# A graph-attention and slice-attention layer on one core: the second MLP as seven block products, the norms inverted as 128x4, the masked logits in one pass, and other turns

## The chip, the cores and the metric

The kernel runs on one core of a Trainium2 chip. The core has five engines with a queue each: TensorE (PE) multiplies matrices into the eight PSUM banks, VectorE (DVE) and ScalarE (ACT) do elementwise work, GpSimd (POOL) does a few small things, and SyncE (SP) issues DMAs. An engine takes its instructions in the order in which they stand in its queue and waits on semaphores for the others. The metric is the device time of one execution in microseconds, lower is better; the median of several runs is given.

## What is computed

The input x has 32 batches of 512 nodes with 256 features, all in float32. One layer has two halves. The first is a graph network with two attention stages; the second, 0/1 adjacency masks only the second stage. The second half is an attention over 64 slices for each of 8 heads. Cut to what matters:

```python
def _gat(inp, adj_mask, W, a):
    h = inp @ W
    f1, f2 = h @ a[:F_, 0], h @ a[F_:, 0]
    e = leaky_relu(f1[:, :, None] + f2[:, None, :], 0.2)
    if adj_mask is not None:
        e = where(adj_mask[None] > 0, e, -9e15)
    return elu(einsum('bij,bjf->bif', softmax(e, axis=2), h))

# first half, on layernorm(x)
out = relu(x @ mlp1_w + mlp1_b)                     # 256 -> 512
out = elu(_gat(out, None, W_fc, a_fc)) + out        # 512
out = relu(out @ mlp2_w + mlp2_b)                   # 512 -> 256: the "second mlp"
out = relu(elu(_gat(out, adj, W_hand, a_hand)) + out)
x = x + out

# second half, on layernorm(x)
w = softmax((x @ W_x @ W_slice) / temp)             # 8 heads x 64 slices
slice_token = einsum('bhnc,bhng->bhgc', x @ W_fx, w) / (w.sum(2)[..., None] + 1e-5)
attn = softmax(q @ k.T * SCALE)                     # from slice_token
x = x + (attn @ v, spread back with w) @ W_out
```

## The kernel before, in words

Each batch is one age of a software pipeline (`nc.age = b`). All its operations are written down by a recorder (`Recorder`) and not emitted at once. `order()` then plays through all 32 ages with a table of costs (`_cost`), and at each step gives every engine the ready operation with the lowest key. The keys come from `TURNS`, one number for each step of a batch (load, norm1, mlp1, h, factors, p, pv, o1, mlp2, h2, e, p2, pv2, norm2, w, sums, s1T, tokens, att, vo, gg, out), with corrections for the first and last three batches in `HEAD` and `TAIL`. The order that comes out is emitted, so that it is fixed when the program is built; up to four batches are under way at a time. All instructions carry the line of the emitting call (L288 in the profile of before), so that groups are told apart by tile names.

A batch has 512 nodes as four tiles of 128 rows. The steps that matter here:

- `h` (line 682): the product of o0T (the first MLP's output, features on partitions) with `wfc` is done as seven block products: four mixtures of o0T in the tile `mix`, three mixtures of the weights in `mixed`, sums of products on DVE into the tile `h`. After it come `factors`, `p` and `pv`: the attention without mask, whose weights lie in `pT`.
- `o1` (line 790): the attention's output goes through DRAM (`gather`: four writes to `scr`, one read of 1 MB) to come back transposed as `o1T`, and o0T is added.
- `mlp2` (line 800): two output tiles of 128 features, each four products of 128x128 weights from `w2` with 512 columns of `o1T`, and one ReLU with bias on ACT into `o2T`.
- `h2` and `e` (lines 810 to 848): `h2` is o2T times `wh`; the two logits columns stand beside it. For each of the four row tiles DVE adds the column logits `f2b`, the row logit and the mask `mbias` (bfloat16), takes the leaky ReLU as max(0.2 e, e), and the row's maximum; ACT takes the exponential. DVE transposes 32x32 blocks into `e_stage`, and a gather through DRAM makes `p2T`.
- `w`, `sums`, `s1T`, `tokens` (lines 908 to 992): w holds the slice weights. `sums` multiplies them with the normalised x, whose last feature is set to 1, so that the last row of `s1T` holds the norms, 512 numbers in one partition. They go to DRAM (`line`) and come back broadcast over partitions as `rn` (128x256), where DVE adds 1e-5 and inverts; `tok` is the tokens' product times `rn`.

A tile that carries a tag shares its buffer with the other tiles of that tag; `bufs` is how many such buffers there are. Each float32 matmul of the program stands as two MATMUL instructions in the profile.

The few lines to have at hand:

```python
pm.rearrange("p (a t i) -> p a t i", t=NT, i=Q), w2[:, k, ts(m)],      # 806
swapped(o1T[:, k, :]), start=(k == 0), stop=(k == KH - 1),              # 807
nc.vector.tensor_scalar(rn, rn, 1e-5, None, op0=OP.add)                 # 974
nc.vector.reciprocal(rn, rn)                                            # 975
```

Of the kernel before, what the change touches and what calls it, by code (L numbers as in the profile page):

```python
# [10 lines left out]
AF = mybir.ActivationFunctionType  # L11
OP = mybir.AluOpType
AX = mybir.AxisListType
# [1 line left out]
ENGINES = ("tensor", "vector", "scalar", "gpsimd", "sync")  # L15

TURNS = {
    "load": -462.5, "norm1": 57.6, "mlp1": 1478.5, "h": 1624.1, "factors": 1626.7, "p": 1631.1,
    "pv": 1644.1, "o1": 1647, "mlp2": 1694.9, "h2": 1709.3, "e": 1714.6, "p2": 1102.3,
    "pv2": 1733.3, "norm2": 1780.6, "w": 1806.7, "sums": 1812.1, "s1T": 1826.8, "tokens": 2321.2,  # L20
    "att": 658.3, "vo": 1004.5, "gg": 1394.8, "out": 1524.2,
}
PERIOD, SPARE = 89.9, 0.01

HEAD = (
    (-33, 108, 3, -726, 0, 63, -4, 93, -317, -118, -101, -31, 114, 36, 581, -77, -43, -443, 55,
     -1, 16, -659),
    (302, 200, 0, 41, 0, 223, 198, 0, -15, 0, 760, -14, -1674, -151, 33, -31, -61, -1067, 191,
     -140, -300, 8),
    (-6, 37, 1179, -81, 0, 0, -1864, -1, 0, 1, -105, -68, -395, 94, 4, -151, 5, 3, -336, 3, 0,  # L30
     0),
)
TAIL = (
    (-203, -62, 1108, 0, -19, -60, 101, 4, -242, -90, -82, 1, -58, -418, -434, 1119, -43, -15,
     -10, 0, -198, 0),
    (295, 0, 75, 221, 12, 158, -7, 50, -1, 64, 0, 173, -8, -61, -5, 0, 30, 0, -59, -299, 730,
     197),
    (94, 1079, -126, 0, -154, 915, -18, 0, 0, -1924, -62, -58, -41, 72, -15, 360, 0, -238, 0,
     -132, -14, 140),
)  # L40


# [3 lines left out]

P = 128
ALPHA = 0.2
MASKED = -4.5e16


class Recorder:
# [3 lines left out]
    SIGNAL = 0.06  # L56
    DRAIN = 0.17
    ISSUE, BEGIN, LAND, BEHIND = 0.45, 2.2, 0.0, 3.6
    SWITCH = 0.1
    KEPT = 1  # L60
    AHEAD = 3

# [65 lines left out]
    def _cost(self, op, out, ins):  # L128


        def words(ap):
            return ap.size() // ap.ap[0][1]

        n = words(out)
        if op.method == "dma_start":
            side = next(ap for ap in (out, *ins) if ap.space != bass.MemoryType.DRAM)
            kb = out.size() / 256
            if side.ap[0][1] <= P // 4:
                op.moving = 0.3 + max(0.0, 1.08 * (kb / 128 - 1))
            else:  # L140
                op.moving = max(1.5 * kb / 512, 4.0 * kb / 1024 - 0.5)
            return self.ISSUE, 0.0
        if op.engine == "tensor":
            one = max(n / 1200 + 0.002, 0.109)
            if op.mode == (P, P // 2):
                one = max(n / 2400, 0.0275)
            elif op.mode == (P // 2, P // 2):
                one = max(n / 4800, 0.0135)
            return (one if op.method == "transpose" else 2 * one), self.DRAIN
        if op.engine == "scalar":  # L150
            pointers = sum(isinstance(op.kwargs.get(k), bass.AP) for k in ("bias", "scale"))
            return 0.06 + n / 1200 + 0.09 * pointers + 0.19 * ("accum_out" in op.kwargs), 0.12
        if op.engine == "vector":
            n = max([n] + [words(x) for x in ins])
            single = op.method in ("tensor_copy", "tensor_scalar")
            fast = single and all(x.space != bass.MemoryType.PSUM for x in ins)
            pointers = sum(words(x) == 1 for x in ins) if n > 1 else 0
            return 0.07 + n / (1920 if fast else 960) + 0.065 * pointers, 0.1
        if n < 16:
            return (0.1 if op.method == "memset" else 0.3 if op.method == "tensor_scalar" else 1.1), 0.1  # L160
        return 0.2 + n / (480 if op.method == "tensor_tensor" else 960), 0.1
# [164 lines left out]
def adj_ffn_kernel(  # L326
# [26 lines left out]
    B, N, D = x.shape  # L353
    HID = mlp1_w.shape[1]
    HH = HID // 2
    NT = N // P
    KD = D // P
    KH = HID // P
# [4 lines left out]
    NP = INNER // P  # L363
    assert G == C == 64 and HEADS * G == 512 and N == 512 and HID == 512 and D == 256

    nc = Recorder(tc.nc)
# [5 lines left out]
    def ts(i, n=P):  # L372
        return slice(i * n, (i + 1) * n)

    def new(name, shape, bufs=1, tag=None, dtype=F32):
        return sbuf.tile(list(shape), dtype, name=name, tag=tag or name, bufs=bufs)

    def mm_tile(shape):
        return psum.tile(shape, F32, tag="bank", name="mm", bufs=8)
# [8 lines left out]
    Q = 32  # L388
# [23 lines left out]
    def swapped(cols):  # L412

        return cols.rearrange("p (t a i) -> p a t i", t=NT, i=Q)
# [4 lines left out]
    def row(name, shape=(P, 512), tag=None):  # L419
        return new(name, shape, bufs=2, tag=tag)  # L420

    def small(name, shape):
        return new(name, shape, bufs=3)
# [8 lines left out]
    def load_x(b):  # L432
# [14 lines left out]
        out=ident, in_=ident, compare_op=OP.not_equal, fill=1.0, base=0,  # L447
# [37 lines left out]
    t1, t2, t4 = (mixed[:, i] for i in range(3))  # L485
    for to, left, right in ((t1, r12, r11), (t2, r22, t1), (t4, r21, t2), (r12, r22, r12)):
        nc.vector.tensor_tensor(to, left, right, op=OP.subtract)
    t3 = r12

    nc.step = "setup"  # L490
    w2 = new("w2", [P, KH, D])
    nc.sync.dma_start(w2, mlp2_w.rearrange("(k p) f -> p k f", p=P))
    b2 = new("b2", [P, KD])
    nc.sync.dma_start(b2, mlp2_b.rearrange("(m p) -> p m", p=P))

# [27 lines left out]
    mbias = new("mbias", [P, NT, N], dtype=BF16)  # L523
# [87 lines left out]
    for p in range(NP):  # L611
        pv = mm_tile([P, D])
# [49 lines left out]
    def front(b):  # L662
# [11 lines left out]
        for m in range(KH):  # L674
            pm = mm_tile([P, N])
# [7 lines left out]

        h = new("h", [P, NT, 2, HH + 1])
        l11, l12, l21, l22 = (o0T[:, ts(k, 2), ts(t, 2 * P)] for t in range(2) for k in range(2))
        mix = new("mix", [P, 4, 2, 2 * P])
        s1, s2, s3, s4 = (mix[:, i] for i in range(4))
        for to, left, op, right in (
            (s1, l21, OP.add, l22), (s2, s1, OP.subtract, l11),
# [32 lines left out]
        f1, f2 = h[:, :, 0, HH], h[:, :, 1, HH]  # L722
# [30 lines left out]
        pT = new("pT", [P, NT, N])  # L753
        for j in range(NT):
# [5 lines left out]
                op0=OP.mult, op1=OP.max,  # L760
# [3 lines left out]
        o1T = new("o1T", [P, KH, N])  # L764
        if by_dma("u", b):
            stage = new("u_stage", [P, HID // Q, P], bufs=2, tag="stage")
        for i in range(NT):
            pms = [mm_tile([P, HH + 1]), mm_tile([P, HH])]
            for s, pm in enumerate(pms):
                for j in range(NT):  # L770
                    nc.tensor.matmul(
                        pm, pT[:, j, ts(i)], h[:, j, s, : HH + 1 - s],
                        start=(j == 0), stop=(j == NT - 1),
# [3 lines left out]
            u, m = row("u"), row("m")  # L777
# [13 lines left out]
        if by_dma("u", b):  # L791
            gather("u", stage, o1T)
            for m in range(KH):
                o1 = o1T[:, m, :].rearrange("p (t a i) -> p t a i", t=NT, i=Q)
# [3 lines left out]
    def middle(b, o1T):  # L798

        nc.step = "mlp2"  # L800
        o2T = new("o2T", [P, KD, N])
        for m in range(KD):
            pm = mm_tile([P, N])
            for k in range(KH):
                nc.tensor.matmul(
                    pm.rearrange("p (a t i) -> p a t i", t=NT, i=Q), w2[:, k, ts(m)],
                    swapped(o1T[:, k, :]), start=(k == 0), stop=(k == KH - 1),
                )
            nc.scalar.activation(o2T[:, m, :], pm, AF.Relu, bias=b2[:, m : m + 1])
        nc.step = "h2"  # L810
        h = new("h2", [P, NT, D + 2], tag="h" if b == B - 1 else None)
        for t in range(NT):
            pm = mm_tile([P, D + 2])
# [5 lines left out]
        f2b = tr_tile([P, N])  # L819
        for j in range(NT):  # L820
            nc.tensor.transpose(f2b[:, ts(j)], h[:, j, D + 1 : D + 2].to_broadcast([P, P]), ident)
        if not by_dma("e", b):
            pt, f2b = f2b, new("f2b", [P, N], tag="acb")
            nc.scalar.copy(f2b, pt)
        nc.step = "e"
        pT = new("p2T", [P, NT, N], tag="pT" if b == B - 1 else None)
        if by_dma("e", b):
            stage = new("e_stage", [P, N // Q, P], bufs=2, tag="stage")
        nmax = small("nmax", [P, NT])
        for i in range(NT):  # L830
            e = new("e", [P, N], bufs=2)
            nc.vector.scalar_tensor_tensor(
                e, f2b, h[:, i, D : D + 1], mbias[:, i, :], op0=OP.add, op1=OP.add
            )
            nc.vector.scalar_tensor_tensor(e, e, ALPHA, e, op0=OP.mult, op1=OP.max)
            nc.vector.tensor_reduce(
                nmax[:, i : i + 1], e, axis=AX.X, op=OP.max, negate=True
            )
            nc.scalar.activation(e, e, AF.Exp, bias=nmax[:, i : i + 1])
            if by_dma("e", b):  # L840
                flip(e, stage[:, :, ts(i, Q)])
                continue
            pt = tr_tile([P, NT, P])
            for j in range(NT):
                nc.tensor.transpose(pt[:, j, :], e[:, ts(j)], ident)
            nc.scalar.copy(
                pT.rearrange("p j (t a i) -> p j t a i", t=NT, i=Q)[:, :, :, i, :],
                pt.rearrange("p j (t i) -> p j t i", i=Q),
            )
# [18 lines left out]
        for i2 in range(NT // 2):  # L868
            parts = []
            for s in range(2):  # L870
                i = 2 * i2 + s
                pm = mm_tile([P, D + 1])
# [7 lines left out]
            u, m = row("u2", (P, 2, D), "u"), row("m2", (P, 2, D), "m")  # L880
# [10 lines left out]
    def back(b, x1):  # L891
# [21 lines left out]
        for t in range(NT):  # L913
            pm = mm_tile([P, INNER])
# [38 lines left out]
        if by_dma("w", b):  # L953
            raw = new("w_raw", [P, NP, N], tag="w")
            gather("w", stage_w, raw)
            for p in range(NP):
                nc.scalar.copy(
                    wT[:, p, :].rearrange("p (t a i) -> p t a i", t=NT, i=Q), swapped(raw[:, p, :])
                )
        nc.step = "s1T"  # L960
        line = dram.tile([NP, 2, G], F32, name="line", tag="line", bufs=2)
        nc.sync.dma_start(
            line.rearrange("(o p) s g -> o (p s g)", o=1), s1T[P - 1 : P, KD - 1, :]
        )
        rn = new("rn", [P, NP, G], tag="mean")
        for s in range(2):
            nc.sync.dma_start(
# [3 lines left out]
                    ap=[[0, C], [2 * G, NP], [1, G]],  # L971
                ),
            )
        nc.vector.tensor_scalar(rn, rn, 1e-5, None, op0=OP.add)
        nc.vector.reciprocal(rn, rn)
        nc.step = "tokens"

        nc.joint = True
# [75 lines left out]
        gg = med("gg")  # L1054
# [93 lines left out]
```

## Time and profile before

| | |
|---|---|
| median of 3 runs | 2535.09 us (2533.92 to 2537.39) |
| the profiled execution | 2531.39 us |
| its span, first to last instruction | 2529.6 us |
| granted TensorE clock | 0.996 |
| HBM | 137 GB/s over the span |
| matmuls of mlp2 (o1T,w) | 512 instructions, 246.8 us busy |
| inversion of rn on DVE | 32 instructions, 56.0 us busy |
| longest DMA kind, w_raw<-scr | 30 transfers of 1024 KB, 7.9 us to landing |

The span is what the hardware profiler saw of one execution; the rest of the 2531.39 us lies around it. A row of a group gives busy time and mean duration of one instruction, then the engine's idle time before it with what ended that. Matmuls overlap in the pipeline, so their durations add up to more than the time they take: the distance between starts is what counts.

### The profile page before, as it was taken

How to read it: one execution, taken by the hardware profiler on the slowest of the kernel's cores; microseconds unless marked ns; L12 is line 12 of the kernel's file. 1: busy time of each engine (PE TensorE's matmuls, PEld its weight loads, DVE VectorE, ACT ScalarE, POOL GpSimd, SP SyncE). 2: the span in 40 equal slices, each digit the busy share in tenths (PEclk: the TensorE clock that was granted, in tenths of full speed). 3: DMA queues.
4: the chain of work that ended last, by engine and by line, in shares of the span. 5: the costliest groups of instructions: out<-in, count | busy, mean ns of one | idle time of the engine just before them, and what ended most of it. 6: DMA issues, size and time to landing. Idle time of an engine off the chain costs nothing.

```text
span 2529.6 us, 33819 instructions
## 1 busy us (share of the span) xinstructions
PE 2487.6 (98%) x11653; PEld 1726.1 (68%) x11653; DVE 2157.7 (85%) x5108; ACT 1059.7 (42%) x1941; POOL 101.1 (4%) x167
## 2 busy tenths in 40 slices
PE   7999999999999999999999999999999999999988
PEld 5767667776667666677666676766676666767655
DVE  7778889988889888889888898888898888888865
ACT  3434343433444434444434434334444344444432
POOL 0000000000000000000000000000000000000000
PEclk9999999999999999999999999999999999999989
DMA  5243456544556544555544565445565445545432
GB/s 162 59 120 94 130 155 169 158 128 127 136 160 170 148 126 131 151 160 160 135 132 128 160 172 148 131 134 136 160 169 144 127 130 155 162 127 148 109 97 63
DMA packets 441985, 348.60 MB, mean 138 GB/s; under 512 B 101044, under 2 KB 366388, under 8 KB 441814
## 3 DMA queue, kind: packets, MB, share of 16 engines
q1 hardware_dynamic: 440230, 345.39, 50.3%
q8 instruction: 93, 1.52, 0.2%
q10 hardware_dynamic: 1584, 1.05, 0.1%
q14 instruction: 78, 0.64, 0.1%
HBM read 186.92 MB, written 159.45 MB: 137 GB/s over the span
## 4 chain that ended last, share of the span: by engine, by line
PE 81%; ACT 6%; DVE 6%; DMA 5%; SPq 1%; issue 1%; POOL 0%; DVEq 0%; ACTq 0%
PE mm L288 79%; ACT pT L288 2%; PE tr L288 2%; DMA rn<-line 2%; ACT acb L288 2%; SPq L288 1%; DMA xn_raw<-scr 1%; ACT o2T L288 1%; DVE rn L288 1%; DVE acb L288 1%; DMA scr<-xn_stage 1%; DVE u L288 1%; DVE h L288 1%; DVE xn_stage L288 1%; DVE xn L288 0%
## 5 line engine op out<-in xcount | busy, mean ns | idle before, releaser
L288 PEld LDWEIGHTS mm<-h,pT 128*128 128x128 f32 x2048 | 385.8, 189 | 152.0 <-issue 87.9
L288 PE MATMUL mm<-h,pT 128*128 128x257 f32 (+1 forms) x2048 | 483.8, 379 | 1.6 <-DVE pT L288 1.6
L288 PE MATMUL mm<-weff,xn2T 128*128 128x512 f32 x512 | 256.3, 607 | 1.7 <-ACT xn2T L288 1.7
L288 PE MATMUL mm<-w,xn 128*128 128x512 f32 x512 | 252.8, 592 | 0.0
L288 PE MATMUL mm<-o1T,w 128*128 128x512 f32 x512 | 246.8, 593 | 0.8 <-DVE o1T L288 0.8
L288 PE MATMUL mm<-xnT,w 128*128 128x512 f32 x512 | 232.3, 603 | 0.7 <-ACT xnT L288 0.7
L288 PE MATMUL mm<-gg,wT 128*128 128x256 f32 x1024 | 230.5, 379 | 0.8 <-DVE gg L288 0.8
L288 PE MATMUL mm<-h,p2T 128*128 128x257 f32 x1024 | 228.2, 380 | 0.0
L288 PEld LDWEIGHTS mm<-gg,wT 128*128 128x128 f32 x1024 | 193.6, 190 | 41.0 <-issue 15.0
L288 ACT ACTIVATE e<-e,nmax 128x512 f32<-128x512 f32 x128 | 92.4, 722 | 294.9 <-DVE nmax L288 294.8
L288 PEld LDWEIGHTS mm<-h,p2T 128*128 128x128 f32 x1024 | 194.0, 190 | 29.4 <-issue 1.2
L288 DVE TENSOR_TENSOR h<-mm,h 128x257 f32<-128x257 f32 x320 | 128.8, 419 | 61.7 <-PE mm L288 61.0
L288 PEld LDWEIGHTS mm<-xnT,w 128*128 128x128 f32 x512 | 95.1, 191 | 107.9 <-issue 102.5
L288 ACT ACTIVATE m<-m 128x512 f32<-128x512 f32 x192 | 120.9, 630 | 112.2 <-DVE m L288 112.2
L288 ACT COPY h<-mm 128x258 f32<-128x258 f32 (+1 forms) x256 | 95.0, 373 | 135.9 <-PE mm L288 135.3
L288 ACT ACTIVATE u<-mm,rd 128x256 f32<-128x256 f32 x192 | 90.3, 470 | 145.0 <-DVE rd L288 68.4
L288 ACT ACTIVATE w<-w 128x512 f32<-128x512 f32 x128 | 80.7, 630 | 162.4 <-DVE w L288 162.2
L288 DVE SCALAR_TENSOR_TENSOR pT<-acb,ex,pT 128x512 f32<-128x512 f32 x128 | 94.0, 745 | 63.8 <-ACT pT L288 63.8
L288 ACT ACTIVATE m<-m,neg 128x512 f32<-128x512 f32 x192 | 138.4, 721 | 5.3
L288 DVE SCALAR_TENSOR_TENSOR u<-m,u 128x512 f32<-128x512 f32 x192 | 129.7, 675 | 11.7 <-ACT m L288 11.5
L288 ACT COPY xn2T<-xn_raw 128x512 f32<-128x512 f32 x60 | 34.2, 615 | 245.9 <-DMA xn_raw<-scr 245.9
L288 PEld LDWEIGHTS mm<-o1T,w 128*128 128x128 f32 x512 | 91.6, 189 | 58.0 <-issue 39.5
(150 smaller groups left out, 4208.8 us busy)
## 6 DMA issues: line engine op xcount, KB each, us to landing
scr<-xn_stage SPq DMA_DIRECT2D x240, 128.0 KB, 2.5
scr<-u_stage SPq DMA_DIRECT2D x120, 256.0 KB, 5.9
o1T<-scr SPq DMA_DIRECT2D x30, 1024.0 KB
scr<-e_stage SPq DMA_DIRECT2D x120, 256.0 KB, 4.9
p2T<-scr SPq DMA_DIRECT2D x30, 1024.0 KB, 5.5
scr<-w_stage SPq DMA_DIRECT2D x120, 256.0 KB, 4.8
w_raw<-scr SPq DMA_DIRECT2D x30, 1024.0 KB, 7.9
x<-in_x_dram SPq DMA_DIRECT2D x32, 512.0 KB
```

Source lines behind the costliest of these rows:

```text
L288: getattr(getattr(self.nc, op.engine), op.method)(*op.args, **op.kwargs)
```

## The change

- `mlp2` is written as seven block products. w2 is split in 2x2 blocks (feature halves k, output halves m), o1T in 2x2 blocks (feature halves k, node halves n). Three mixtures of the weights lie in the new tile `mixed2`, others in w2's own place; they are made once, in the setup. Per batch four differences of o1T blocks go into `mix2`, which takes the buffer of `p2T`; seven products of 256 columns with two matmuls each are summed on DVE, and the ReLU is done in place on four blocks of o2T.
- `mix` of the step `h` takes the buffer of `pT`.
- In `e` the mask and the row's maximum are one instruction, on the logits before the row logit and the leaky ReLU are applied. ACT then takes two exponentials, one for each branch of the leaky ReLU, and DVE the larger.
- The norms are brought from the one row to a 128x4 tile `norm`, inverted there, written to `line`, and broadcast as `rn`. The inversion of the 128x256 tile goes.
- All numbers in `TURNS`, `HEAD` and `TAIL`, and four in the cost table, are others.

```diff
-PERIOD, SPARE = 89.9, 0.01
+PERIOD, SPARE = 90.53, 0.01
...
-MASKED = -4.5e16
+MASKED = -(2.0 ** 55)
...
-    SWITCH = 0.1
+    SWITCH = 0.17
...
-                one = max(n / 4800, 0.0135)
+                one = max(n / 4000, 0.0135)
...
+            if op.method == "reciprocal":
+                return 0.05 + n / 145, 0.1
...
+    mixed2 = new("mixed2", [P, 3, 2, P])
+    w2_11, w2_12, w2_21, w2_22 = (w2[:, ts(k, 2), ts(m)] for m in range(KD) for k in range(2))
+    m1, m2, m4 = (mixed2[:, i] for i in range(3))
+    for to, left, op, right in (
+        (m1, w2_21, OP.add, w2_22), (m2, m1, OP.subtract, w2_11), (m4, w2_12, OP.subtract, m2),
+        (w2_21, w2_11, OP.subtract, w2_21),
+    ):
+        nc.vector.tensor_tensor(to, left, right, op=op)
+    m3 = w2_21
+    nc.vector.tensor_scalar(w2_22, w2_22, -1.0, None, op0=OP.mult)
...
-        mix = new("mix", [P, 4, 2, 2 * P])
+        mix = new("mix", [P, 4, 2, 2 * P], tag="pT")
...
-        for m in range(KD):
-            pm = mm_tile([P, N])
-            for k in range(KH):
-                nc.tensor.matmul(
-                    pm.rearrange("p (a t i) -> p a t i", t=NT, i=Q), w2[:, k, ts(m)],
-                    swapped(o1T[:, k, :]), start=(k == 0), stop=(k == KH - 1),
-                )
-            nc.scalar.activation(o2T[:, m, :], pm, AF.Relu, bias=b2[:, m : m + 1])
+        o11, o12, o21, o22 = (o1T[:, ts(k, 2), ts(n, 2 * P)] for k in range(2) for n in range(2))
+        mix = new("mix2", [P, 4, 2, 2 * P], tag="p2T")
+        t1, t2, t3, t4 = (mix[:, i] for i in range(4))
+        for to, left, right in ((t1, o12, o11), (t2, o22, t1), (t4, t2, o21), (t3, o22, o12)):
+            nc.vector.tensor_tensor(to, left, right, op=OP.subtract)
+
+        def product(left, right):
+            pm = mm_tile([P, 2 * P])
+            for k in range(2):
+                nc.tensor.matmul(pm, left[:, k, :], right[:, k, :], start=(k == 0), stop=(k == 1))
+            return pm.rearrange("p (t a i) -> p t a i", t=2, i=Q)
+
+        def part(m, n):
+            return o2T[:, m, :].rearrange("p (a t i) -> p t a i", t=NT, i=Q)[:, ts(n, 2)]
+
+        def total(to, left, right):
+            nc.vector.tensor_tensor(to, left, right, op=OP.add)
+
+        c11, c12, c21, c22 = (part(m, n) for m in range(2) for n in range(2))
+        nc.scalar.copy(c12, product(w2_11, o11))
+        total(c11, product(w2_12, o21), c12)
+        nc.scalar.copy(c22, product(m1, t1))
+        total(c12, product(m2, t2), c12)
+        total(c21, product(m3, t3), c12)
+        total(c12, c12, c22)
+        total(c22, c21, c22)
+        total(c12, product(m4, o22), c12)
+        total(c21, product(w2_22, t4), c21)
+        for m, n, c in ((0, 0, c11), (1, 1, c22), (0, 1, c12), (1, 0, c21)):
+            nc.scalar.activation(c, c, AF.Relu, bias=b2[:, m : m + 1])
...
-        nmax = small("nmax", [P, NT])
-        for i in range(NT):
-            e = new("e", [P, N], bufs=2)
-            nc.vector.scalar_tensor_tensor(
-                e, f2b, h[:, i, D : D + 1], mbias[:, i, :], op0=OP.add, op1=OP.add
-            )
-            nc.vector.scalar_tensor_tensor(e, e, ALPHA, e, op0=OP.mult, op1=OP.max)
-            nc.vector.tensor_reduce(
-                nmax[:, i : i + 1], e, axis=AX.X, op=OP.max, negate=True
-            )
-            nc.scalar.activation(e, e, AF.Exp, bias=nmax[:, i : i + 1])
+        f1, top, low = h[:, :, D], small("top", [P, NT]), small("low", [P, NT])
+        masked = [new("e", [P, N], bufs=4) for i in range(NT)]
+        for i, e in enumerate(masked):
+            nc.vector.tensor_tensor_reduce(
+                out=e, in0=f2b, in1=mbias[:, i, :], scale=1.0, scalar=3.0 * MASKED,
+                op0=OP.add, op1=OP.max, accum_out=top[:, i : i + 1],
+            )
+        nc.vector.tensor_tensor(top, top, f1, op=OP.add)
+        nc.vector.scalar_tensor_tensor(top, top, ALPHA, top, op0=OP.mult, op1=OP.max)
+        nc.vector.scalar_tensor_tensor(low, f1, ALPHA, top, op0=OP.mult, op1=OP.subtract)
+        nc.vector.tensor_tensor(top, f1, top, op=OP.subtract)
+        for i, e in enumerate(masked):
+            above = row("above", tag="m")
+            nc.scalar.activation(above, e, AF.Exp, bias=top[:, i : i + 1])
+            nc.scalar.activation(e, e, AF.Exp, scale=ALPHA, bias=low[:, i : i + 1])
+            nc.vector.tensor_tensor(e, e, above, op=OP.max)
...
+        norm = new("norm", [P, NP], bufs=2)
+        nc.sync.dma_start(norm, s1T[P - 1 : P, KD - 1, :])
+        nc.vector.tensor_scalar(norm, norm, 1e-5, None, op0=OP.add)
+        nc.vector.reciprocal(norm, norm)
         line = dram.tile([NP, 2, G], F32, name="line", tag="line", bufs=2)
-        nc.sync.dma_start(
-            line.rearrange("(o p) s g -> o (p s g)", o=1), s1T[P - 1 : P, KD - 1, :]
-        )
+        nc.sync.dma_start(line.rearrange("p s (q f) -> (p s q) f", f=NP), norm)
...
-        nc.vector.tensor_scalar(rn, rn, 1e-5, None, op0=OP.add)
-        nc.vector.reciprocal(rn, rn)
```

## The prediction

> **What bounds the kernel now.** I read the page's busy shares first, then busy time in a stretch from the middle, then the chain of waits (for the period), then the timeline of one period, then the groups.
>
> ```profile
> PE 2487.6 (98%) x11653; PEld 1726.1 (68%) x11653; DVE 2157.7 (85%) x5108; ACT 1059.7 (42%) x1941; POOL 101.1 (4%) x167
> ...
> 1200.00:1600.00 400.00, 398.95 (x1850) 275.16 (x1848) 345.98 (x822) 167.84 (x308) 15.96 (x25) 1.00 0.52 143
> ...
> 377.00 64.83 PE mm L288 x298
> ...
> 1991.97 64.83 PE mm L288 x298
> ```
>
> In the middle stretch (PE, PEld, DVE, ACT, POOL) PE is busy 99.7% at full clock, DVE 86%, ACT 42%. The two pieces of the chain are the same place 21 batches apart: (1991.97 - 377.00)/21 = 76.9 us a batch. 32 x 76.9 = 2461; the other 69 us of the span of 2529.6 are the head and the tail.
>
> ```profile
> 1281.62 1.03 PE L288 MATMUL mm<-wfc,mix 128*128 128x257 f32 x4
> 1282.49 1.02 PE L288 MATMUL mm<-o1T,w 128*128 128x512 f32 x2
> 1283.35 1.03 PE L288 MATMUL mm<-mixed,o0T 128*128 128x257 f32 x4
> ...
> 1284.42 0.43 DVE L288 TENSOR_TENSOR h<-mm,h 128x257 f32<-128x257 f32 x1 [0.59 <-PE mm L288]
> 1286.14 0.42 DVE L288 TENSOR_TENSOR h<-mm,h 128x257 f32<-128x257 f32 x1 [1.30 <-PE mm L288]
> ...
> 1292.88 0.75 DVE L288 SCALAR_TENSOR_TENSOR pT<-acb,ex,pT 128x512 f32<-128x512 f32 x1 [2.63 <-ACT pT L288]
> ```
>
> Starts, not durations, give the price on PE: two 512-wide matmuls in 0.86 us, four 257-wide in 0.87. Over the whole trace the median distance of starts is 0.429 for 512 columns, 0.216 for 257 and 0.2155 for 256. All matmuls of a batch at these distances (and the small ones at their measured sums) come to 75.6 us, so only 1.3 us of a batch's 76.9 is PE waiting or switching. Any PE work removed must show, unless a new wait eats it. The DVE rows show where DVE has room: it waits 0.6 to 2.6 us at a time while mlp2 and wh run.
>
> **What the Trainium skill says.** "TensorE: Matmul & The Clock Gate", Part 1 ("Wait — 56ns, not 53.3ns?"): starts of warm matmuls lie N/2.4 GHz plus 2.5 ns apart, so time goes by columns with hardly a fixed cost. The trace agrees for halving: 0.429 against 2 x 0.2155. The paragraph on queue depths in its section "Architectural detail" has LDWEIGHTS pulled ahead of running matmuls; here a load takes 189 ns, below the 215 ns of a 256-wide matmul, and gg<-wT already runs that way. "VectorE: DVE Perf Modes", tier table: fp32 tensor_tensor has only the 1x mode; the trace has 0.68 us for 512 elements, from SBUF or PSUM. "DMA: Bandwidth & Descriptors", Anatomy of one DMA: about 2 us fixed for a transfer. The line DMA here took 2.1 us (issued 2501.80, its reader 2503.94).
>
> **The change, per batch.** *PE.* Removed: 8 products of 512 columns, two instructions each: 16 x 0.429 = 6.86 us. Added: 7 block products of two matmuls at 256 columns, 28 x 0.2155 = 6.03. Gain 0.83 us, times 32 = 26.6 us. Nothing else on PE changes in number.
>
> *DVE.* Rows used:
>
> ```profile
> L288 DVE TENSOR_REDUCE nmax<-e 128x1 f32<-128x512 f32 x128 | 87.0, 681 | 0.0
> L288 DVE SCALAR_TENSOR_TENSOR e<-tr,h,mbias 128x512 f32<-128x512 f32 x120 | 86.2, 739 | 3.8 <-PE tr L288 3.8
> L288 DVE SCALAR_TENSOR_TENSOR e<-e 128x512 f32<-128x512 f32 x128 | 84.2, 678 | 0.0
> L288 DVE RECIPROCAL rn<-rn 128x256 f32<-128x256 f32 x32 | 56.0, 1751 | 0.9
> L288 DVE DVE_READ_ACCUMULATOR m<-wfc,ab 128x1 f32 x8 | 0.7, 84 | 0.0
> ```
>
> Removed: 4 x (0.739 + 0.678 + 0.681) = 8.39, and on rn 0.294 + 1.751 = 2.05; together 10.4. Added: four o1T differences 4 x 0.68 = 2.72; seven sums of 256 at 0.42 = 2.94; four fused mask-and-maximum passes, each with a read of the accumulator; four 128x4 operations, 0.8 at most (the ex row has 0.223); four maxima 4 x 0.68 = 2.72; on norm 0.15 + 0.17 (the ra reciprocal on 128x4). The trace has no fused pass: at best a plain pass of 0.68, at worst two rows' worth, 1.4. I take 0.74 + 0.08, the row with the same operands, 3.3 in all. Sum 12.8, net +2.4 us. DVE goes from 86.5% of 76.9 (66.5 us) to 69 of 76.1, 91%: still not the bound on average; with the bad price 71.6, 94%.
>
> *ACT.* Four more exponentials at 0.72, two copies at 0.37, four ReLUs of 256 (0.45 from the 256-wide rows) for two of 0.682: +4.1 us, 32 to 36 of 76. Hidden by its own idle time.
>
> *SP.* One more issue (norm), about 0.3 us, but a third hop: s1T row to norm, DVE inverts, norm to line, line to rn. In the SP order as built, line now waits for DVE's reciprocal and stands ahead of the xn_stage writes and of xn_raw; xn_raw has its slack (its readers are ACT copies before weff, some 12 us of PE work later). The hop costs 2.1 to 2.5 us (the xn_stage write's median) and gives back 2.05 of DVE: near nothing where it is exposed, in the last batch (+1).
>
> *Buffers.* mix in pT's place: its first write comes some 10 us of PE work after the last pv matmul that reads pT. mix2 in p2T's: the last p2T read is 9.7 us of PE work before the first product of h (16 matmuls of w and xnT with the sums' 1.15 between), the first mix2 write later still. Cost nothing; if pv ran 10 us late they would bind.
>
> *Order.* All the turns differ, and the built order no longer repeats every batch but every second. In one kind of batch mlp2 comes in the midst of h's products, so DVE must do the sums of h, the o1T additions, mix2 and the sums of mlp2 in one stretch. Count from the first h product. PE: 36 narrow matmuls x 0.216 + 2 = 8.2 us to mlp2, then 28 x 0.2155, four of weff (1.72), and two each of wqk, wfc and wh: the second k of wh, which needs all of o2T, is due at 17.2. DVE: last pv2 product 9.7 us before; elu, residual, norm and flips of it some 12 us (the same rows 1262.4 to 1278 in the trace, less what lies between), so free at about +2.4 with norm inverted; three mix 1.8, two sums 0.7, four o1T 2.4, one sum, three mix2 1.8: tok at 9.45. After tok: 0.37, mix 0.6, thirteen 256-wide at 0.35, mx and w 1.2, fm 0.1 = 6.8, then the ReLU 0.55: wh can start at 16.9. It fits by 0.35 us. In the other kind tok has until 15.3.
>
> Tok waits for rn. norm is inverted at 2.4, line lands 0.4 + 2.5 later, rn is issued at 5.3. The tail shows what rn takes alone and behind a 1 MB transfer:
>
> ```profile
> 2477.72 0.38 SPq L288 DMA_DIRECT2D w_raw<-scr  x1
> 2478.16 1.24 SPq L288 DMA_DIRECT2D rn<-line  x2
> ...
> 2501.80 0.23 SPq L288 DMA_DIRECT2D line<-s1T  x1
> 2503.94 1.24 SPq L288 DMA_DIRECT2D rn<-line  x2
> ```
>
> Its DVE reader began at 2507.67, 3.7 us after the issue, in the second; the chain puts 6.11 us of DMA from 2478.80 in the first, 6.7 from the issue. So rn is there at 9.0 or at 12.0. In the changed order the 1 MB (o1T) goes out before line, hence mostly done: I take 9.0, no stall, and keep 12.0 for the range. Behind tok in DVE's queue stand mix2's last block and the sums that free the PSUM banks.
>
> *Sum.* PE -26.6; the thin fits, 0.1 us a batch, +3; head and tail +2 (five setup operations on w2, 2 us of DVE beside a waiting PE; in the last batch mlp2's DVE work +4, rn hop +1, the masked step 4 x 0.68 less before its exponentials). -21.6 on the profiled execution (2531.39, span 2529.6) gives 2509.8; the median shown is 2535.09, so 2513.5; I say 2514.
>
> **Rivals.** (1) *The new turns also take waits away.* For: 1.3 us a batch is lost now, the largest part before weff and wh. Against: DVE is fuller and two fits are thin. A quarter of it, 0.3 x 32 = 10, and a tighter tail by 4: about 2500. (2) *Half the gain goes into DVE.* More sums per product make banks come free later, and the fused pass costs 1.4: 0.4 us more waiting a batch, 13: 2526; at 0.7 a batch no change is measured. (3) *Slower: tok holds DVE.* If rn comes at 12.0, wh starts at 12.0 + 7.4 = 19.4, 2.2 us late, in every second batch: 16 x 2.2 = 35, -26.6 + 35 + 2 = +10: 2545. It decides from rn at 11.5, where 16 x 1.66 eats 26.6. For: rn after w_raw did take 6.7. Against: the row of sums is ready long before, and 5 us lie between o1T's issue and rn's. (4) *The fused pass does not do its maximum with the sum*, being another instruction: then its price alone changes; it is inside (2).
>
> **How the numbers follow.** Forecast 2514 (0.44), rival 1 0.14, rival 2 0.22 (0.05 of it within 0.2%), slower by rival 3 0.20. What a measurement here can tell from no change is about 0.2%, 5 us. Faster 0.75, same 0.05, slower 0.20. Range: from 2500 (rival 1) to 2540, which leaves out most of rival 3 and the best of rival 1; the likeliest alone spans 2506 to 2522.
>
> **What would show it.** Right: o1T,w, mixed and mix2 products at 256 columns, 896 in all, with starts 0.215 apart; the chain's pieces 76.1 us apart (or 152.2 over two batches); DVE near 90%; fused passes of 0.7 us. Wrong: periods of 77 or more; PE idle before wh with ACT o2T or DVE tok as releaser; long DVE waits for rn<-line. Then rival 3 holds. If the period is right and the time isn't, it lies in the head or the tail.

## The result, and the profile after

| | before | after |
|---|---|---|
| median | 2533.92 us of 9 runs (2530.09 to 2537.79) | 2527.50 us of 9 runs (2524.48 to 2529.44) |
| ratio after / before | | 0.997, 95% interval 0.996 to 0.998 |
| profiled execution, its span | 2531.39, 2529.6 us | 2525.80, 2524.0 us |
| granted TensorE clock | 0.996 | 0.994 |

The change made the kernel faster by 6.4 us, where 21.6 had been forecast: the sign is right, the size less than a third. 2527.5 lies within the stated range of 2500 to 2540, but above the 2506 to 2522 of the likeliest case.

The page's busy shares and the same stretch from the middle as before (columns: stretch, then PE, PEld, DVE, ACT, POOL):

```profile
PE 2470.2 (98%) x12037; PEld 1797.5 (71%) x12037; DVE 2193.6 (87%) x5593; ACT 1175.2 (47%) x2197; POOL 96.3 (4%) x167
...
1200.00:1600.00 400.00, 396.92 (x1927) 290.03 (x1926) 355.66 (x901) 187.74 (x353) 15.40 (x25) 1.00 0.52 146
```

DVE rose from 346.0 to 355.7 us in this stretch, 89%, and PE fell from 398.95 to 396.92: it waits more. The period, from two pieces of the chain of waits twenty batches apart:

```profile
462.70 65.47 PE mm L290 x310
...
1993.68 65.52 PE mm L290 x310
```

(1993.68 - 462.70)/20 = 76.55 us a batch. Before it was 76.9, and 76.1 had been forecast. The groups of the new work (busy time, mean ns of one, idle before it):

```profile
L290 DVE CUSTOM_DVE_ANT_0 e<-tr,mbias 128x512 f32<-128x512 f32 x120 | 81.1, 681 | 2.6 <-PE tr L290 2.5
L290 DVE DVE_READ_ACCUMULATOR2_ANT top<- 128x1 f32 x128 | 10.7, 83 | 0.0
L290 DVE TENSOR_TENSOR o2T<-mm,o2T 128x256 f32<-128x256 f32 x160 | 66.7, 420 | 42.5 <-ACT o2T L290 32.8 <-PE mm L290 7.3
L290 DVE RECIPROCAL norm<-norm 128x4 f32<-128x4 f32 x32 | 5.0, 157 | 0.2
L290 PE MATMUL mm<-mix,w 128*128 128x256 f32 x256 | 71.1, 384 | 5.1 <-ACT o2T L290 5.0
```

The fused mask and maximum is one pass of 681 ns and a read of 83. What is new in the last two columns is ACT o2T: DVE's sums wait for it, and so does PE.

**Where the expected gain went.** The starts of the matmuls tell it more exactly than busy times. For each matmul I took the distance to the next start, and took from it the median distance of its shape (0.429, 0.216, 0.2155 us and so on): what is left is a stall. (Another average for the small products shifts the stalls of both kernels alike and leaves the differences.) Cut at the first wvo,mean product of the fourth and of the 28th batch:

| us | before: work, stalls | after: work, stalls | stalls more |
|---|---|---|---|
| head, to batch 4 | 426.5, 20.9 | 422.8, 34.4 | +13.5 |
| middle, 24 batches | 1796.4, 32.5 | 1790.2, 41.7 | +9.2 |
| tail | 214.6, 25.9 | 197.9, 24.1 | -1.8 |
| sum | 2437.4, 79.3 | 2410.9, 100.2 | +20.9 |

PE's work fell by 26.5 us, as forecast. 20.9 us came back as stalls, and -26.5 + 20.9 = -5.6 is the difference of the two spans. In the middle the 192 changes between tile shapes cost 23 us in both kernels; the rest of the stalls went from 9.2 to 18.3, and 6.3 of these stand in one place, nine times 0.7 us on the average, between the products mix,mixed and mix,w of the second mlp. The answers for PE's waits, summed over the execution (us, times, longest), after:

```profile
PE tr L290 <- DVE wx L290: 7.7, 1, 7.7
PE mm L290 <- ACT o2T L290: 5.2, 10, 1.1
PE tr L290 <- DVE fm L290: 2.8, 1, 2.8
```

Before:

```profile
PE tr L288 <- DVE wx L288: 2.3, 1, 2.3
PE tr L288 <- DVE fm L288: 0.3, 1, 0.3
```

No row for ACT o2T stands in the list of before. (wx are the weights W_x, fm is a maximum over batch 0's logits.) One of the ten as a chain of waits (start, us):

```profile
580.04 5.19 DMA scr<-u_stage
...
589.64 0.09 DVE norm L290
589.73 0.03 DVE h L290
589.76 5.84 DMA line<-norm
...
595.61 0.59 SPq L290
...
597.02 4.38 DMA xn_raw<-scr
...
601.42 0.02 ACT xn2T L290
601.45 0.50 issue
601.95 0.62 ACT xn2T L290
602.57 0.02 issue
602.59 0.38 ACT o2T L290
602.97 0.04 issue
603.02 4.57 PE mm L290 x16
```

Read from below: PE's mix,w waits for a copy of o2T on ACT, the first of the new mlp. That copy is late because two copies of xn2_raw, the other batch's normalised x, stand ahead of it in ACT's queue. These wait for the transfer xn_raw, which waits on SP behind rn, and rn behind line. line took 5.84 us from issue. SP's queue shows what had gone out just before it:

```profile
588.63 0.38 SPq L290 DMA_DIRECT2D o1T<-scr  x1
589.76 0.35 SPq L290 DMA_DIRECT2D line<-norm  x1
590.15 0.93 SPq L290 DMA_DIRECT2D scr<-xn_stage  x2
595.61 1.25 SPq L290 DMA_DIRECT2D rn<-line  x2
597.02 0.49 SPq L290 DMA_DIRECT2D xn_raw<-scr  x1
```

2 KB went out 1.1 us behind o1T's 1 MB. This is so in every second batch: the 12 lines that were issued 0.5 to 1.1 us behind o1T took 5.3 to 6.7 us to landing, the 12 that were issued 5 to 7 us behind it 1.8 to 3.9 us. The median over all, 3.1 us, mixes the two kinds; o1T's is 7.4.

### The profile page after: what moved, and what is told of

Read it like the earlier page. It is cut to its first block, busy times and chain, and to the rows that moved or that the text cites. A ratio compares the mean times of both kernels' runs of the same rounds, so it can differ in the third digit from the quotient of the medians.

```text
span 2524.0 us, 35133 instructions
## 1 busy us (share of the span) xinstructions
PE 2470.2 (98%) x12037; PEld 1797.5 (71%) x12037; DVE 2193.6 (87%) x5593; ACT 1175.2 (47%) x2197; POOL 96.3 (4%) x167
## 4 chain that ended last, share of the span: by engine, by line
PE 77%; DMA 9%; DVE 8%; ACT 3%; SPq 1%; issue 1%; POOL 0%; DVEq 0%; ACTq 0%
PE mm L290 74%; PE tr L290 3%; DMA line<-norm 2%; DMA xn_raw<-scr 2%; DMA scr<-u_stage 1%; SPq L290 1%; DVE mix L290 1%; DVE u L290 1%; ACT m L290 1%; DVE xn_stage L290 1%; DVE xn L290 1%; DMA p2T<-scr 1%; DVE m L290 1%; DMA scr<-xn_stage 0%; DMA w<-in_L_gnn_mlp_w_dram 0%
## 5 line engine op out<-in xcount | busy, mean ns | idle before, releaser
L290 PE MATMUL mm<-h,pT 128*128 128x257 f32 (+1 forms) x2048 | 478.5, 379 | 1.3 <-DVE pT L290 1.3
L290 PE MATMUL mm<-h,p2T 128*128 128x257 f32 x1024 | 242.6, 380 | 1.0 <-DMA p2T<-scr 1.0
L290 ACT COPY h<-mm 128x257 f32<-128x257 f32 (+1 forms) x256 | 95.1, 374 | 130.4 <-PE mm L290 126.2
L290 ACT ACTIVATE o0T<-mm,b 128x512 f32<-128x512 f32 x128 | 87.7, 685 | 106.3 <-PE mm L290 105.6
L290 PEld LDWEIGHTS mm<-w,xn 128*128 128x128 f32 x512 | 94.9, 189 | 57.1 <-issue 44.0
L290 PE MATMUL mm<-wfc,mix 128*128 128x257 f32 x512 | 133.1, 380 | 0.0
L290 PE MATMUL mm<-mixed,mix 128*128 128x257 f32 x512 | 125.0, 384 | 0.1
```

Source lines behind the costliest of these rows:

```text
L290: getattr(getattr(self.nc, op.engine), op.method)(*op.args, **op.kwargs)
```

## The experiments

All are the changed kernel in its own order, except where the text says otherwise; an edit of order is put in after the order has been worked out, so that all else keeps its place. Each is given as its ratio to the kernel before, run on the same chip.

**1. The numbers alone.** The kernel before's TURNS, PERIOD, HEAD and TAIL in the changed program.

```diff
-PERIOD, SPARE = 90.53, 0.01
+PERIOD, SPARE = 89.9, 0.01
...
```

> The changed program with the turns, head, tail and period numbers of the kernel before. Shows what the new numbers are worth. If the program itself gains and the new numbers lose in the head (theory A), the waits before batch 3's last stage come back to 21-25 us and the time lies below 2527.5, near 2518; if the old numbers don't fit the new program, the middle waits more than 2.5 us a batch and the time is over 2540.

3097.3 us, 1.222 (1.220 to 1.224). The old numbers don't fit the changed program; an undone part without new numbers is no fair comparison, so the other runs keep the order. What each of the change's parts is worth alone was therefore not measured.

**2. xn_raw ahead of rn on SP.**

```diff
+if op writes xn2_raw by DMA: put it ahead of the two rn transfers on sync
```

> Same program as the changed kernel and the same order on every engine, but on SP xn_raw's DMA is issued ahead of the two rn DMAs, so that it does not wait behind line's landing. Theory A (the steady loss is a queue on SP: o1T's 1 MB ahead of line, line ahead of rn, rn ahead of xn_raw, whose ACT copies stand ahead of mlp2's first ACT copies): PE's wait between the mix,mixed and mix,w products (0.29 us a batch) goes, the period falls from 76.5 by 0.2 to 0.4 us, the time by 6 to 12 us to 2516-2522. Theory B (DVE is too full in the stretch with h's sums, o1T and mlp2's sums): nothing on DVE changes, so within 2 us of the changed kernel's 2527.5.

2540.7 us, 1.0023 (1.0013 to 1.0032): slower than the changed kernel by 13 us, which neither theory had. xn_raw went out only 0.9 us sooner (its own xn_stage writes queue behind o1T too), and rn then went out behind 512 KB: DVE's tok waited for it 40.8 us in all, against 4.5 in the changed kernel. PE's waits in its profile:

```profile
PE mm L301 <- ACT o2T L301: 19.5, 20, 2.2
```

and between mix,mixed and tok,wqk the middle's starts lost 12.7 us, ten times, where the changed kernel lost 0.3. One of the ten:

```profile
600.44 0.43 DVE L301 TENSOR_TENSOR tok<-mm,rn 128x256 f32<-128x256 f32 x1 [1.08 <-DMA rn<-line]
601.38 0.70 PE L301 MATMUL mm<-tok,wqk 128*128 128x256 f32 x2 [1.25 <-ACT o2T L301]
```

tok, held by rn, was ready at 600.87, and PE went on only when ACT's first copy of o2T had ended, at 601.34. Eight of the ten waits end with this copy, one with tok. In this trace tok,wqk waits here for ACT's semaphore, in the changed kernel only for PE's own, though PE, DVE and ACT run the same order in both; that another PSUM bank was given to the product would explain it, and is not shown. So the run changed a second thing: it says little on theory A, and how much of its 13 us is tok held by rn, rival 3's mechanism, stays open.

**3. Less work on DVE at the same place.** Three quarters of the o1T additions are left out.

```diff
-nc.vector.tensor_tensor(o1, o1, swapped(o0T[:, m, :]), op=OP.add)
+nc.vector.tensor_tensor(o1[:, :, 0:1], o1[:, :, 0:1], swapped(o0T[:, m, :])[:, :, 0:1], op=OP.add)
```

> The order of the changed kernel, but the four additions of o0T to o1T (0.68 us each, in the stretch where DVE is fullest) do only a quarter of their columns, three quarters are left out: 4 x 0.47 = 1.9 us less on DVE a batch. Theory B (DVE too full there): the waits of PE fall by 0.4 us a batch or more, the span to 2512 or less. Theory A (queue on SP): only the wait before mlp2's first product (0.16 us a batch) goes, the xn_raw wait stays: span 2518-2524.

Span 2528.4 us in a single execution, against 2524.0. 1.6 us less DVE work a batch gave nothing. The wait for o1T's additions went (3.4 us to 0), and this took its place:

```profile
PE mm L292 <- ACT o2T L292: 11.9, 13, 1.3
```

So DVE's fullness, the reason in rival 2, is not what binds here: PE gets there sooner and waits for ACT longer.

**4. The small transfers on another queue.**

```diff
-nc.sync.dma_start(norm, ...)      # and line, rn
+nc.scalar.dma_start(norm, ...)
```

> The changed program in the same order; the four small transfers of the norms (norm, line, two rn) are issued by ACT's queue in place of SP's. Theory L (the third hop that the change put on SP's queue is what delays xn2_raw and rn: line lands 5.8 us after its issue, since it queues behind o1T's 1 MB): line lands within 3 us, xn2_raw is issued 0.5 to 1 us sooner, PE's waits between mix,mixed and mix,w fall from 6.4 to about 3 us, the median to 2522 to 2526. Rival M (xn2_raw waits for the writes of xn_stage, which queue behind o1T as well; and ACT now waits for norm's inversion and for line): the median is 2527 to 2540 with ACT waiting for DMA line in the trace.

2548.1 us, 1.0052 (1.0034 to 1.0070). Slower, with the waits moved again (the first number is us in total):

```profile
ACT xn2T L292 <- DMA rn<-line: 59.6, 7, 8.9
DVE norm L292 <- DMA norm<-s1T: 22.3, 14, 4.3
PE mm L292 <- DVE tok L292: 9.0, 15, 1.2
```

The stalls between mix,mixed and mix,w fell from 6.3 to 1.4 us, more than theory L had; but norm went out later behind ACT's work, and DVE, which has no time to give, stood before it (4.1 us in the changed kernel). Now PE waits for DVE's tok, as in rival 3, and for mix (6.1 us). Nor did the other queue make line quick where it matters: issued from ACT's queue 1.8 to 2.5 us behind o1T, six of them took 4.6 to 5.7 us to landing. (The trace tells 24 of the 32 landings.) So the slow landing goes with the 1 MB under way at that time, and not with the place behind it in SP's queue.

**5. The buffer and the order on ACT.** xn2_raw shares o2T's buffer, so even with another order ACT could not write o2T first. A first form let q share tokT's buffer, to make room, also in the planning; with that the whole order came out anew.

> The changed program in the same order; xn2_raw gets a buffer of its own in place of o2T's (q takes tokT's for that). Theory J (the two share a buffer, so o2T's first copy can't be written before xn2_raw is read): only a part of the wait goes, since ACT's queue still has the copies of xn2_raw ahead: PE's waits between mix,mixed and mix,w stay near 6 us over 24 batches and the median within 3 us of 2527.5. If they fall below 3 us, the buffer alone was the bound.

> As own_raw, and where ACT's two copies of xn2_raw stand ahead of the two copies of mlp2's products, they are put behind them. Theory J (mlp2 hangs on xn2_raw by ACT's queue and the buffer): PE's waits between mix,mixed and mix,w fall from 6.4 us to under 1.5 over the 24 middle batches, and the median by 4 to 6 us, to 2522 to 2524. Rival K (PE then waits a moment later for weff's xn2T, which comes 1 us later): the waits move to mix,w to weff,xn2T, and the median stays at 2526 to 2529.

3024.2 and 3028.4 us: both say only what run 1 said. The second form keeps the order:

```diff
-raw = new("xn2_raw", [P, KD, N], tag="o2T")
+raw = new("xn2_raw", [P, KD, N])
-q = new("q", [P, 2, 2, G])
+q = new("q", [P, 2, 2, G], tag="tokT")
+# planned as if the tags were the old ones
```

> The changed program in the same order on every engine; xn2_raw gets a buffer of its own in place of o2T's. Theory J (mlp2's first copies hang on xn2_raw by ACT's queue, which has its two copies ahead): the buffer alone changes little, PE's waits between mix,mixed and mix,w stay at 4 to 7 us over the 24 middle batches, the median within 3 us of 2527.5. If they fall below 3 us, the shared buffer alone was the bound.

2523.4 us, 0.9967 (0.9954 to 0.9980), the ratio of the changed kernel; the stalls between mix,mixed and mix,w fell from 6.3 to 4.0 us. The buffer alone is at most a part. Then, with it, the order on ACT:

```diff
-scalar.copy xn2T, scalar.copy xn2T, scalar.copy o2T, scalar.copy o2T
+scalar.copy o2T, scalar.copy o2T, scalar.copy xn2T, scalar.copy xn2T
```

> As own_raw2, and on ACT the two copies of xn2_raw come behind mlp2's two copies where they stood ahead. Theory J: PE's waits between mix,mixed and mix,w fall from 6.4 us to under 1.5, the median by 3 to 6 us, to 2522 to 2525. Rival K (PE waits a moment later instead, for xn2T or for DVE's sums): the same time is lost between mix,w, weff and wh, and the median stays at 2526 to 2529.

2512.7 us (2511.4 to 2515.3), 0.9924 (0.9909 to 0.9939): about twice the expected gain (12.8 us by the spans of the profiled executions), and the fastest kernel of the study, 0.76% faster than the one before. ACT at the same place of the same batch (in brackets the idle time before, and what ended it), first the changed kernel, then this:

```profile
601.42 1.14 ACT L290 COPY xn2T<-xn_raw 128x512 f32<-128x512 f32 x2 [10.05 <-DMA xn_raw<-scr]
602.59 0.65 ACT L290 COPY o2T<-mm 128x256 f32<-128x256 f32 x2
```

```profile
596.69 0.37 ACT L304 COPY o2T<-mm 128x256 f32<-128x256 f32 x1 [7.68 <-PE mm L304]
598.41 0.37 ACT L304 COPY o2T<-mm 128x256 f32<-128x256 f32 x1 [1.35 <-PE mm L304]
598.68 1.14 ACT L304 COPY xn2T<-xn_raw 128x512 f32<-128x512 f32 x2
```

In the changed kernel both copies wait until the transfer is there, 4.7 us after the first product began (597.89 on PE); here the first comes 1.2 us after it (595.52). The chain of waits in this stretch has lost its DMA pieces:

```profile
544.04 54.76 PE mm L304 x240
598.81 0.03 issue
598.84 5.44 PE mm L304 x20
```

The middle's stalls are 32.95 us, against 41.67, and 32.46 before the change. No row of ACT o2T is left among PE's waits. Of the 8.7 us won, 6.3 stood before mix,w and 1.1 each at the next two places of mlp2. So what the middle had lost on balance came from this one chain, of queue order and buffer together; the order can't be had without the buffer. The waits that are left are not those of before: 7.9 us at wh have gone, and others have come. In this run too tok,wqk waits for ACT's semaphore at this place; PE loses nothing there.

**6. Was the chain there before?** The same edit in the kernel before (with r2's buffer, which is free then).

> The kernel before, all of its work, with the same edit as own_act2: xn2_raw leaves o2T's buffer (for r2's, which is free then), and ACT's first ReLU of mlp2 comes ahead of the two copies of xn2_raw. Theory N (the chain over xn2_raw hurts only since mlp2's products are seven, whose sums build on the first copies; before, PE could go on to the second output tile): it gains little here, the median within 4 us of before, 2528 to 2534. Rival O (the chain was there before and the change only kept it): it gains as much as in the changed kernel, 8 to 12 us, to 2521 to 2525.

2529.3 us, 0.9978 (0.9970 to 0.9987): 5.6 us by the ratio, between the two theories; own_act2 gains 0.46%, 11.7 us, on the changed kernel. The trace doesn't show where: the middle's stalls fell only from 32.5 to 31.0, against 8.7 us there, and the profiled execution is the second slowest of 12, with a span 1.2 us above that of before. So the edit helps the kernel before, too, about half as much by the times; that it is the same chain is not shown. Why the chain should cost more now is argued only: before, the ReLU that stands behind xn2_raw closes one of two products, and PE waits for it at wh; after, two copies open a row of sums, and the products that follow need banks which only these sums free.

**7. The head.** The theory: on DVE, setup work stands ahead of batch 0. PE's waits in the first 120 us of the changed kernel, beside those for wx (7.7 us) and fm (2.8) that are shown above:

```profile
PE tr L290 <- DVE xn L290: 8.6, 1, 8.6
PE mm L290 <- DMA xnT<-scr: 1.4, 1, 1.4
```

The first is also there before. Each edit below moves whole instructions in the first 50 to 120 us only.

```diff
-w2's mixtures, wfc's logits, wh's logits, mask, W_fx, W_x, batch 0's mixtures and sums
+head_late:  ..., batch 0's mixtures, W_fx, W_x, then its sums
+head_first: wfc's logits, batch 0's mixtures, wh's logits, mask, w2's mixtures, W_fx, W_x between the sums
+head_two:   as head_first; rows of W_fx and W_x ahead of W_out; factors straight after the sums
+both:       own_act2 and head_two; batch 1's first mlp later
+both4:      as both; attention products ahead of the transposes of u
+both5:      as both4; the norms of batches 2 and 3 later
```

> The changed kernel's order, but in the setup the work on W_fx, W_x and the weights made from them stands behind the mixtures and products of batch 0's h on DVE, PE and ACT. Theory A (the turns put wx's transposes ahead of batch 0's products, PE waits 7.7 us for loads that come late, and this is never made good): the waits before batch 3's last stage fall from 34.4 us by 6 to 9, the time to 2518-2521. Rival (the first batches are bound by their own chains, the wait is absorbed there): within 2 us of 2527.5.

> The changed program, all of its work; only the order of the first 50 us is another: batch 0's mixtures and products of h come first, the mixtures of w2, the logits columns of wh, the mask, and the work on W_fx and W_x stand behind or between its sums, and the setup's products on PE behind all products of h, much as in the kernel before. Theory H (the head lost 13.5 us to setup work that got ahead of batch 0 on DVE): PE's stalls up to batch 3 fall from 34.4 to some 24 us, the wait for wx from 7.7 to under 3, and the median to 2516 to 2520. Rival I (the head only fills a pipeline that later waits anyway): the stalls turn up again before batch 5, and the median stays at 2525 to 2529.

> The changed program, all of its work. As head_first, and besides the rows of W_fx and W_x are fetched ahead of W_out's four transfers, batch 0's factors come straight after its sums of h on DVE, and batch 1's norm and first mlp behind batch 0's attention weights, as in the kernel before. Theory H: PE's stalls up to batch 3 fall from 34.4 to 20 to 25 us (before: 20.9) and the median to 2514 to 2520. Rival I (what the head wins is lost again where the pipeline fills, since the later order was made for the late start): the waits for wx and fm go, but the stalls of batches 1 to 4 grow by as much, and the median is 2525 to 2530.

> The changed program, all of its work, with own_act2's buffer and ACT order and head_two's order of the first 50 us, except that batch 1's first mlp comes behind 14 of 16 attention products of batch 0 in place of 8 (head_two waited 8.2 us there for xnT). If theory J and theory H are both right the gains add: stalls up to batch 3 fall from 32.2 (own_act2) to 22 to 26 us, the middle stays at 33, and the median falls from 2512.7 to 2503 to 2507. If the head's gain is lost again where the pipeline fills (rival I): 2511 to 2515, with the stalls of batches 1 to 4 larger.

> The changed program, all of its work, with own_act2's buffer and ACT order, and the first 80 us in the order of the kernel before: as 'both', and besides batch 0's attention products run on PE ahead of the transposes of its output, batch 1's norm stands on DVE between batch 0's first elu and the rest, batch 2's and 3's norms behind batch 0. If the head's loss is an order that can be mended (theory H): stalls up to batch 3 fall from 32 (own_act2) to 22 to 26 us and the median to 2502 to 2508. If they stay at 30 or more, a third place of waiting has taken over, and the head's loss belongs to the way the batches enter the new order (rival I); the median is then 2510 to 2516.

> The changed program, all of its work: both4, whose wait of 13.1 us before mix2 came from the norms of batches 2 and 3 ahead of batch 0's second mlp on DVE; here batch 2's norm stands behind that mlp and batch 3's behind batch 1's attention weights. In both4 PE had lost 15.1 us by 78 us, against 22.9 in own_act2. Theory H (order alone): that lead of 8 us holds, stalls up to batch 3 are 23 to 27 us, the median 2503 to 2508. Rival I: another wait follows before batch 3, stalls 30 us or more, the median 2510 to 2520; then the loss of the head isn't settled by these orders.

| run | ratio (interval) | stalls to batch 4 | the new wait |
|---|---|---|---|
| changed kernel | 0.9970 (0.996 to 0.998) | 34.4 | |
| head_late | 0.9976 (0.9969 to 0.9983) | 36.9 | wx for b_x 6.1, mix 5.3 |
| head_first | 0.9995 (0.9985 to 1.0004) | 40.2 | fm 9.2 |
| head_two | 0.9972 (0.9962 to 0.9983) | 33.8 | xnT 8.2 |
| own_act2 | 0.9924 (0.9909 to 0.9939) | 32.2 | |
| both | 0.9948 (0.9933 to 0.9963) | 38.7 | u 3.2 and 7.9 |
| both4 | 0.9948 (0.9931 to 0.9965) | 43.2 | mix2 12.9 |
| both5 | 0.9946 (0.9928 to 0.9963) | 42.4 | h 4.2, xn 5.8 |

The wait for wx fell as meant, from 7.7 us to 2.0 in head_two. But six orders out of six gave it back elsewhere, most of them in a place that my own edit had made:

```profile
PE mm L375 <- DVE mix L375: 13.5, 2, 12.9
```

That is both4, where two norms stood ahead of the second mlp. both5 moved only these; some 65 us into the span PE had lost 14.5 us, 8 less than own_act2, and by batch 4 it had lost 10 more than own_act2. A long wait has a second price here. The window view of both5 (stretch; PE, PEld, DVE, ACT, POOL; then the granted clock):

```profile
92.00:96.00 4.00, 1.22 (x3) 1.03 (x4) 2.60 (x12) 2.25 (x5) 0.00 (x0) 0.77 0.60 130
96.00:100.00 4.00, 4.00 (x11) 3.17 (x10) 3.99 (x10) 3.63 (x6) 0.00 (x0) 0.50 0.75 261
100.00:104.00 4.00, 4.00 (x20) 2.87 (x19) 2.61 (x8) 1.29 (x3) 0.00 (x0) 0.88 0.02 5
```

After a wait of 4.2 us, which ended at 94.78, 13 matmuls started at twice their distance, 2.8 us more. The Trainium skill ("TensorE: Matmul & The Clock Gate", Part 1) has the array's clock halved after an idle window, and some 3.4 us of steady work to bring it back. The trace agrees on the half; the full clock was back 6.2 us after the wait's end here, and 3.7 to 6.4 us after thirteen single waits of 4.2 to 12.9 us in the heads of these runs. Over the head such matmuls make 4.8 us of the changed kernel's stalls and 10.6 of both5's. In the kernel before they make 5.2, so they are no part of what the change lost in the head.

Not all of the head's loss arises where these edits work. At 78 us PE had lost 21.8 us in the changed kernel and 13.2 before, 8.6 more. Some 4 us more come between 200 and 300 us, in five waits of 0.5 to 1.9 us (for mean, gg, w, pT and o0T), and no edit reaches these.

What stays open: whether another order of the head would win its 13.5 us back. With wx's wait at 2.0 us the head lost as much as ever, but each edit made a wait of its own, so no run separates the causes. That the loss is bound to the way in which the batches enter the new order is what fits, and not shown.

## Why the prediction was wrong

**Right.** The 896 block products stand in the trace, 256 columns each, and PE's work fell by 26.5 us for 26.6. The fused pass is the cheap one, 0.68 + 0.08 for 0.74 + 0.08. ReLUs of 256 took 0.504 for 0.45. DVE is at 89% in the middle for 91%, and no average bound. Rival 3 did not come, since rn was early enough: DVE's tok waited 4.5 us for rn in the whole execution. Run 4, where PE waits 9.0 us for tok, shows how near it was.

**The step that failed: "the thin fits, 0.1 us a batch, +3; head and tail +2".** Measured, +9.2 for the middle and +11.7 for the ends. The sign of being wrong that was named, PE idle with ACT o2T as releaser, is there, but before mix,w and not before wh.

The middle fell by a sentence about SP: "xn_raw has its slack (its readers are ACT copies before weff, some 12 us of PE work later)". I looked for the last use of xn2_raw, weff. Its readers stand in ACT's queue ahead of the first copies of mlp2, and share their buffer; so the slack was that of o2T's copies, not of weff. For the added hop I named what is queued behind it on SP, and did not follow that on to what is queued behind the reader on ACT. Where I looked for the thin place, at wh, 9.2 us of waits in 24 batches became 1.2. The second part is the hop: "line lands 0.4 + 2.5 later" measured 5.84 us at this place, and 5.3 to 6.7 in every batch of its kind. The forecast knew that o1T's 1 MB goes out before line and took it for mostly done: it had been issued 1.1 us earlier.

In the head, "five setup operations on w2, 2 us of DVE beside a waiting PE" was put at nothing: the other parts of the term (+4, +1, -2.7) already make its +2. They waited 3.0 us for w2 at the head of DVE's queue, and the order behind them put some 9 us of setup between batch 0's first and second mixture (16.71 and 30.66 on DVE, the rest being wfc's logits and a wait for W_fx), so PE, which has wx's transposes ahead of the later products of h, stood 7.7 us before wx and 2.8 before fm. These places are shown; that an order without them would win the time is not. The diff shows that all turns differ; I had not followed the built order of the first 50 us on DVE. The tail gave 1.8 back.

Rival 2 (2526) named nearly the time, and not the cause: the 0.4 us more a batch are there (0.38), but less DVE work didn't help in the one execution of run 3, and own_act2 with the same DVE work has them back.

With the chain taken away the sum closes but for the head: own_act2's span is 18.4 us below that of before, and PE -26.5, middle +0.5, head +11.3, tail -3.4 make -18.1. It took an edit that the change did not have.

## What to carry to other kernels

When work is taken from a bound engine and its successor needs an answer from a side engine, look at what stands ahead of that answer in the side engine's queue, whatever its share of busy time: ACT was 53% idle, and two copies for another batch in its queue, with the buffer that they shared, cost 12 us. A buffer shared by tag can fix such an order where nothing in the dataflow does. And a reader's slack ends at the first instruction behind it in its queue, not at the first use of what it writes.

## What the runs showed of the hardware

- A transfer of 2 KB issued 0.5 to 1.1 us behind one of 1 MB on the same queue took 5.3 to 6.7 us to landing, in each of 12 batches; issued 5 to 7 us behind it, 1.8 to 3.9 us. From ACT's queue, 1.8 to 2.5 us behind the 1 MB on SP's, it took 4.6 to 5.7 us.
- After thirteen single waits of 4.2 to 12.9 us (with no other over 0.3 us behind them) PE started its matmuls at twice their distance until 3.7 to 6.4 us later, at a granted clock of 0.50 in the window shown, so that each wait cost 1.2 to 2.8 us beyond itself.
- The fused mask and maximum on DVE costs a plain pass, 681 ns for 512 columns out of PSUM, and a separate read of 83 ns.
